# Four graph layers on one core: layer 0 without GpSimd's clearing, with signs and products a step later, and the last stores of each layer among the next layer's chunks

## The chip, the cores and the metric

The kernel runs on one core of a Trainium2 chip. A core has TensorE (matrix products; PE in the profile, PEld for its weight loads), VectorE (DVE), ScalarE (ACT), GpSimd (POOL) and SyncE (SP), each with a queue of instructions of its own that is worked through in order. Transfers are issued from the queues of SyncE and ScalarE (SPq and ACTq), a few from GpSimd. The metric is the device time of one execution in microseconds.

## The reference

x has 2708 nodes with 512 features; adj is a symmetric 2708 x 2708 matrix of int32 zeros and ones, about 2.4% ones, with ones on its diagonal. Four layers follow each other, each as x = x + layer(relu(layernorm(x)), adj):

```python
# layer 0, h = relu(layernorm(x))
out0 = relu((a.T @ h @ weight) * clip(a.sum(axis=0), 1)**-0.5)
# layer 1: each node takes its first 64 neighbors
keep = (A > 0) & (cumsum(A > 0, axis=1) <= 64)
nb_mean = keep @ h / max(keep.sum(axis=1), 1)
out1 = leaky_relu(h @ W_line.T + b_line) + leaky_relu(nb_mean @ W_nb.T + b_nb)
# layer 2: attention with 8 heads of 64 features, scores f1[n] + f2[m] where adj is set
# layer 3
out3 = relu(concat(h @ W_self + b_self, agg @ W_nb + b_nb) @ W_comb + b_comb)   # agg: mean over neighbors
```

## The kernel before, in words

Nodes are cut into 22 chunks of 126 rows (R), the last one of 62. A tile of features is a chunk by 512. Every layer begins with a dense part over the 22 chunks: load x, normalize it (VectorE's statistics, ScalarE's root), transpose it on TensorE, take relu while ScalarE copies it out of PSUM (hT), multiply by a weight. The helper `dense` gives these as stages of lags 0 to 3, and `staged` traces, for each step, every stage at its lag: load of chunk c, normalization of c-1, transposes of c-2, product of c-3. The product is kept in two parts (`halves`), so that it can be multiplied in reduced precision twice. Then comes the aggregation: columns of the adjacency matrix go in six groups of 4, 4, 4, 4, 3 and 3 chunks, and for each group all 22 row chunks are walked. A pair (g, m) of group and row chunk is a unit; a unit multiplies the halves of chunk m with the adjacency block, 2 products of 512 columns for each chunk of the group, into one PSUM tile per chunk (acc).

Layer 0 does more in its units, since it also makes what the other layers read:

- `load0` loads the block adj[m, group] as int32 into ai, four buffers deep, on SyncE's queue; for the last row chunk it first lets GpSimd clear the tile.
- `count0` (lag 3) makes ar, the block in fp32r, on VectorE (L411), for the products; ab, the block in bf16, on ScalarE (L413), two buffers deep, whose last two columns GpSimd clears (L414), since the transposing product always loads 128 columns; the running count of neighbors cum with a scan on VectorE (L418); the degree up to here, a copy of cum's last column by GpSimd (L426); and the sign of 64 neighbors less the count (L428, ScalarE), summed over the row, from which the index of the last neighbor that counts (last) is found.
- `multiply0` (lag 4) has the products with acc (L330), the transposing products of ab (L456, vT_ps), whose column of ones gives the degree by column (L459, VectorE) and whose rest ScalarE copies to vT as int8 (L468). At the middle of a group it loads the x of the group's chunks. After the last row chunk it evicts each acc: relu and scale by VectorE or ScalarE (y, L480 and L489), the sum with x by GpSimd (L492), and the store to x1 on ScalarE's queue (L99, in `move`).

During group 0 the dense part of layer 0 runs in the same steps. Between layers 0 and 1 the index last is spread over rows: 22 transposes on TensorE (L532) and copies by ScalarE to lastr (L538). Layer 1's dense part writes x1 again with its own-node term, its aggregation (`aggregate`, L330 again, with kt from lastr and vT) ends each chunk in `after1`, with a sum by GpSimd (L582) and a store to x2 on ScalarE's queue. Layer 2's dense part takes x2; there ScalarE also normalizes (hn, L199). Tiles of x come from one ring of six buffers (`load_x`); in layer 2 `count_neighbors` uses the same ring for masks, four for each of 13 row chunks. y, hn and evicted tiles share a ring of three (tag "t").

All this is traced in the order of the program, but the order within each queue is set at build time by a planner that takes ready instructions by their place in the program and the times that it expects. PSUM has eight tiles, which acc, vT_ps and the dense parts share.

Of the kernel before, what the change touches and what calls it, by code (L numbers as in the profile page):

```python
# [8 lines left out]
F32 = mybir.dt.float32  # L9
F32R = mybir.dt.float32r  # L10
BF16 = mybir.dt.bfloat16
I32 = mybir.dt.int32
# [32 lines left out]
def fast_layers(  # L45
# [43 lines left out]
    def rows(c):  # L89
        return min(R, N - c * R)  # L90
# [283 lines left out]
    with ExitStack() as ring_ctx:  # L374
# [2 lines left out]
        w0s = load_weight(weights, w0, "w0s", tag="w")  # L377
        h0 = {}
        l1_weights = []

        def product0(c, xc, hT, n):
            po = ps.tile([P, D], F32, name="h0_ps", tag="ps")
# [3 lines left out]
        with tc.tile_pool(name="l0", bufs=2) as wk:  # L386
# [3 lines left out]
            def load0(i):  # L390
                g, m = units[i]
                if i == 2 * NC:
                    l1_weights.extend(
                        load_weight(weights, w, name, tag="w")
                        for w, name in ((w_nb1T, "wn"), (w_line1T, "wl"))
                    )
                cs, n, gw = groups[g], rows(m), width(groups[g])
                ai = wk.tile([R, WG], I32, name="ai", bufs=4)
                block = adj[m * R : m * R + n, cs[0] * R : cs[0] * R + gw]
                if m == NC - 1:  # L400
                    nc.gpsimd.memset(ai[:, :gw], 0)
                    move(nc.sync, ai[TAIL : TAIL + n, :gw], block)
                move(nc.sync, ai[:n, :gw], block)
                tiles[i] = ai

            def count0(i):
                g, m = units[i]
                cs, n, gw, ai = groups[g], rows(m), width(groups[g]), tiles[i]
# [4 lines left out]
                nc.scalar.activation(ab[:n, :gw], ai[:n, :gw], AF.Square)  # L413
                nc.gpsimd.memset(ab[:n, gw : KR + P - R], 0.0)  # L414
                if gw < KR:
                    nc.vector.memset(ar[:, gw:KR].bitcast(F32), 0.0)
                cum = wk.tile([R, WG], I16, name="cum")
# [18 lines left out]
                tiles[i] = ar, ab  # L436

            def multiply0(i):
# [36 lines left out]
                for k, c in enumerate(cs):  # L475
# [14 lines left out]
                            r[:n], acc.pop(c)[:n], AF.Relu, scale=nrm[:n, k : k + 1]  # L490
                        )
                    nc.gpsimd.tensor_tensor(xc[:n], xc[:n], r[:n], ALU.add)  # L492
# [33 lines left out]
        nc.vector.tensor_scalar(last, last, float(N), 0.5, op0=ALU.add, op1=ALU.mult)  # L526

        lastr = wk.tile([R, NC * R], I16, name="lastr")
        for k in range(0, NC, KMAX):
            pt = ps.tile([P, KMAX * R], F32, name="last_ps", tag="ps")  # L530
            for c in range(k, min(NC, k + KMAX)):
                nc.tensor.transpose(  # L532
                    pt[:R, (c - k) * R : (c - k + 1) * R],
                    last[:R, c : c + 1].to_broadcast([R, R]),
                    ident[:R, :R],
                )
            w = (min(NC, k + KMAX) - k) * R
            nc.scalar.copy(lastr[:, k * R : k * R + w], pt[:R, :w])  # L538
# [34 lines left out]
        def after1(c, acc, xc):  # L573
# [229 lines left out]
    with ExitStack() as stack:  # L803
# [128 lines left out]
        def count_neighbors(i):  # L932
# [809 lines left out]
```

## Time and profile before

| | us |
|---|---|
| time, median of three runs (1892.21 to 1899.74) | 1899.61 |
| span of the profiled execution | 1891.6 |
| layer 0, group 0 with the dense part (52 to 182) | 130 |
| layer 0, groups 1 to 5 (182 to 424) | 242 |
| layer 1, dense part to 593, aggregation to 812 | 388 |
| layer 2 | 812 to about 1480 |
| layer 3 | about 1480 to 1891 |
| TensorE busy over the span | 1801.5 (95%) |

A row of the costliest groups gives the line of the kernel, engine, operation, output and inputs with their shapes, the number of executions; then the busy time and the mean of one in ns; then the time that the engine sat idle just before, and what ended most of it. A row of the timeline gives start and length in us, the engine, line, operation, output and input, the count, and in brackets the idle time before it with what released it. A transfer's row lasts as long as its issues stand on the queue, waits between them included.

### The profile page before, as it was taken

The page shows a single profiled execution, that of the slowest core. Times are in us where ns is not written, and L with a number is a line of the kernel's source. Part 1 is how long each engine was busy: PE and PEld are TensorE (multiplying, and loading weights), DVE is VectorE, ACT ScalarE, POOL GpSimd, SP SyncE. Part 2 cuts the span into 40 slices and gives each one's busy share as a digit, 9 for nine tenths or more (in the row PEclk, how much of TensorE's full clock was granted, in tenths as well). Part 3 has the DMA queues.
Part 4 walks back from the last instruction along what each step waited for, and adds up shares of the span by engine and source line. Part 5 has one row for each costly group of instructions (what it writes and reads, how often), then busy time and mean ns, then how long its engine had stood idle before and what let it go on. Part 6 is the DMA issues. An engine that isn't in the chain of part 4 may idle for free.

```text
span 1891.6 us, 30561 instructions
## 1 busy us (share of the span) xinstructions
PE 1801.5 (95%) x11670; PEld 1061.5 (56%) x11670; DVE 1289.1 (68%) x1812; ACT 903.2 (48%) x1533; POOL 280.9 (15%) x461
## 2 busy tenths in 40 slices
PE   8999899989999999989899999999999799999998
PEld 4556666664446888744344453444444355478886
DVE  4655677784444556766799979999999776524333
ACT  2445777772110000047587898767777766400000
POOL 0101232331111111237600000000000222100000
PEclk9999999999999999989999999999999899999999
DMA  6333455542223111243311212211211444302321
GB/s 221 115 87 96 140 149 154 142 117 73 75 68 97 44 44 47 76 136 107 101 46 34 57 46 57 59 39 29 59 31 41 123 137 137 97 20 81 115 65 41
DMA packets 126041, 160.92 MB, mean 85 GB/s; under 512 B 57406, under 2 KB 77994, under 8 KB 125002
## 3 DMA queue, kind: packets, MB, share of 16 engines
q1 hardware_dynamic: 106764, 123.40, 22.8%
q10 hardware_dynamic: 18544, 33.37, 5.3%
q0 software_dynamic: 576, 2.10, 0.3%
q8 instruction: 94, 1.54, 0.3%
q14 instruction: 63, 0.52, 0.1%
HBM read 111.23 MB, written 47.42 MB: 84 GB/s over the span
## 4 chain that ended last, share of the span: by engine, by line
PE 74%; DVE 7%; DMA 5%; issue 5%; ACT 5%; POOL 2%; SPq 0%; ACTq 0%; DVEq 0%; POOLq 0%
PE acc L330 27%; PE av L882 15%; PE nb_ps L182 8%; PE sums L882 5%; DVE t L858 4%; PE self_ps L182 4%; PE line_ps L182 4%; PE h_ps L182 4%; PE wh_ps L182 3%; DMA ai<-in_adj 2%; PE hT_ps L210 2%; DMA x<-x 1%; DVE cum L418 1%; POOL x L492 1%; ACT sign L428 1%
## 5 line engine op out<-in xcount | busy, mean ns | idle before, releaser
L858 DVE SCALAR_TENSOR_TENSOR t<-rb,ec,vT 126x2708 f32<-126x2708 f32 (+2 forms) x220 | 528.1, 2467 | 25.2 <-ACT b L843 11.0
L882 PE MATMUL av<-t,whs 126*32 126x451 f32 (+4 forms) x4576 | 443.1, 518 | 8.6 <-ACT whs L831 7.4
L330 PE MATMUL acc<-halves,kt 126*126 126x512 f32 x1848 | 430.5, 394 | 1.1 <-DVE kt L1096 1.1
L330 PEld LDWEIGHTS acc<-halves,kt 126*126 126x126 f32 x1848 | 344.0, 186 | 85.6 <-DVE kt L1096 1.2
L843 ACT ACTIVATE b<-t,eb 126x2708 bf16<-126x2708 f32 (+5 forms) x130 | 272.5, 2096 | 39.5 <-DVE t L858 38.4
L882 PEld LDWEIGHTS av<-t,whs 126*32 126x32 f32 (+1 forms) x4576 | 170.6, 110 | 202.0 <-issue 159.8
L330 PE MATMUL acc<-halves,ar 126*126 126x512 f32 x924 | 254.1, 415 | 8.9 <-ACT ab L413 4.3
L330 PEld LDWEIGHTS acc<-halves,ar 126*126 126x126 f32 x924 | 166.5, 189 | 52.8 <-issue 11.6
L563 DVE SCALAR_TENSOR_TENSOR kt<-lastr,index,vT 126x504 fp32r<-126x504 int16 (+1 forms) x132 | 104.3, 798 | 82.1 <-PE acc L330 81.8
L1096 DVE CAST kt<-vT 126x504 fp32r<-126x504 int8 (+1 forms) x132 | 52.7, 400 | 140.8 <-PE acc L330 140.8
L191 ACT ACTIVATE ln_rs<-ln_mv,eps 126x1 f32<-126x1 f32 x88 | 25.5, 294 | 257.6 <-DMA x<-x 202.8
L418 DVE TENSOR_TENSOR_SCAN cum<-ai,deg 126x504 int16<-126x504 int32 (+2 forms) x110 | 125.0, 1143 | 26.9 <-DMA ai<-in_adj 13.9
L784 POOL TENSOR_SCALAR z<-y 126x512 f32<-126x512 f32 x22 | 43.1, 1957 | 646.6 <-DVE y L777 578.2
L428 ACT ACTIVATE sign<-cum,limit 126x504 bf16<-126x504 int16 (+3 forms) x132 | 88.5, 671 | 59.2 <-DVE cum L418 53.9
L882 PE MATMUL sums<-t,whs 126*32 126x339 f32 (+3 forms) x1152 | 107.7, 455 | 5.7 <-ACT out L921 5.7
L831 ACT ACTIVATE whs<-wh,ef 126x64 f32<-126x64 f32 x220 | 73.7, 341 | 69.4 <-PE sums L882 35.5
L212 ACT ACTIVATE hT<-hT_ps 128x504 f32<-128x504 f32 x88 | 51.4, 587 | 103.4 <-PE hT_ps L210 99.4
L187 DVE BATCH_NORM_STATS2 ln_st<-x 126x6 f32<-126x512 f32 x88 | 60.4, 687 | 58.2 <-DMA x<-x 46.0
L468 ACT CAST vT<-vT_ps 126x504 int8<-126x504 f32 (+1 forms) x132 | 70.9, 539 | 47.4 <-DVE sums L459 24.1
L182 PE MATMUL nb_ps<-wn,hT 128*126 128x512 f32 x176 | 81.9, 609 | 2.6 <-ACT hT L212 2.6
L182 PE MATMUL wh_ps<-w2s,hT 128*126 128x512 f32 (+1 forms) x176 | 80.9, 603 | 0.0
L182 PE MATMUL nb_ps<-wfn,hT 128*126 128x512 f32 x176 | 80.4, 600 | 0.0
(172 smaller groups left out, 2054.2 us busy)
## 6 DMA issues: line engine op xcount, KB each, us to landing
x<-x SPq DMA_DIRECT2D x105, 252.0 KB
x<-x ACTq DMA_DIRECT2D x84, 252.0 KB
ai<-in_adj SPq DMA_DIRECT2D x84, 248.1 KB
x<-in_x SPq DMA_DIRECT2D x42, 252.0 KB
rb<-rT SPq DMA_DIRECT2D x7, 1332.8 KB
wh<-whd SPq DMA_DIRECT2D x70, 94.5 KB
whd<-wh SPq DMA_DIRECT2D x21, 252.0 KB
aT<-avT SPq DMA_DIRECT2D x21, 252.0 KB
```

The lines of the kernel that those rows point to most:

```text
L182: nc.tensor.matmul(po[:n], lhsT[:, f, :n], w[:, f, :], start=(f == 0), stop=(f == NF - 1))
L187: nc.vector.bn_stats(st[:n], xc[:n])
L330: nc.tensor.matmul(acc[:R], weight[:, k * R : (k + 1) * R], parts[:, i, :], start=(m == 0 and i == 0), stop=(m == NC - 1),)
L418: nc.vector.tensor_tensor_scan(cum[:n, :gw], ai[:n, :gw], ai[:n, :gw], 0.0 if g == 0 else deg[:n, m : m + 1], op0=ALU.add, op1=ALU.max,)
L428: nc.scalar.activation(sign[:n, :gw], cum[:n, :gw], AF.Sign, bias=limit[:n], scale=-1.0, accum_out=signs[:n, m, g : g + 1],)
L468: nc.scalar.copy(vT[g][:, :, m * R : (m + 1) * R], pt[:R, :K, :R])
L563: nc.vector.scalar_tensor_tensor(by_chunk(kt, cs), lastr[:, cs[0] * R : (cs[-1] + 1) * R].rearrange("p (c r) -> p c r", r=R), index[:R, m ...
L831: nc.scalar.activation(t[:q, :O], wh.pop((u, m))[:q], AF.Copy, scale=by)
L843: nc.scalar.activation(b[:q, : hi - lo], weight[s][:q, : hi - lo], AF.Sigmoid, bias=eb[:q, m, h : h + 1], scale=STEEP,)
L858: nc.vector.scalar_tensor_tensor(t[:q, : hi - lo], row[h][:q, lo:hi], ec[:q, m, h : h + 1], vT[g][:q, k, lo:hi], op0=ALU.max, op1=ALU.mult,)
L882: nc.tensor.matmul(p[j * S : j * S + lhsT.shape[1], : b - a], lhsT, rhs[:, part * size + a : part * size + b], start=(m == 0), stop=(m == ...
L1096: nc.vector.tensor_copy(by_chunk(kt, cs), pattern(m, cs))
```

## The change

In layer 0 the block is loaded two columns wider where there are any, so that ab's two extra columns are made by ScalarE with the rest and GpSimd clears them only in the last group. ai goes from four buffers to five, ab from two to three. The copy of the degree moves from GpSimd to VectorE. The sign is written over cum and goes into a stage of its own. Counts, signs and products have lags 4, 5 and 6, where counts had 3 and products 4. The sums of a group are kept (`sums1`), and their stores to x1 are traced in the steps of row chunks 1 to 4 of the next group; those of the last group among the chunks of layer 1's dense part, those of layer 1's last group among layer 2's. The spreading of last goes among layer 1's chunks too. To make room, the ring of x has five buffers, not six. The purpose is that ScalarE's queue does not hold stores that wait for GpSimd in front of work that TensorE needs, and that GpSimd's adds do not hold ab.

```diff
-    def load_x(src, c, name="x", pool=None, bufs=6, twice=False):
+    def load_x(src, c, name="x", pool=None, bufs=5, twice=False):
...
+        def save2(c):
+            move(nc.scalar, x2[c * R : c * R + rows(c), :], sums1.pop(c)[: rows(c)])
+        def save1(c):
+            move(nc.scalar, x1[c * R : c * R + rows(c), :], sums1.pop(c)[: rows(c)])
...
-                ai = wk.tile([R, WG], I32, name="ai", bufs=4)
+                wide = min(gw + P - R, N - cs[0] * R)
+                ai = wk.tile([R, WG + P - R], I32, name="ai", bufs=5)
...
-                ab = wk.tile([R, WG + P - R], BF16, name="ab")
-                nc.scalar.activation(ab[:n, :gw], ai[:n, :gw], AF.Square)
-                nc.gpsimd.memset(ab[:n, gw : KR + P - R], 0.0)
+                ab = wk.tile([R, WG + P - R], BF16, name="ab", bufs=3)
+                nc.scalar.activation(ab[:n, :wide], ai[:n, :wide], AF.Square)
+                if wide < KR + P - R:
+                    nc.gpsimd.memset(ab[:n, wide : KR + P - R], 0.0)
...
-                nc.gpsimd.tensor_copy(deg[:n, m : m + 1], cum[:n, gw - 1 : gw])
-                sign = wk.tile([R, WG], BF16, name="sign", bufs=1)
+                nc.vector.tensor_copy(deg[:n, m : m + 1], cum[:n, gw - 1 : gw])
+                tiles[i] = ar, ab, cum
+
+            def sign0(i):
...
                 nc.scalar.activation(
-                    sign[:n, :gw],
+                    cum[:n, :gw],
                     cum[:n, :gw],
                     AF.Sign,
...
-                    move(nc.scalar, x1[c * R : c * R + n, :], xc[:n])
+                    sums1[c] = xc
+
+            def save0(i):
+                g, m = units[i]
+                if g and 1 <= m <= len(groups[g - 1]):
+                    save1(groups[g - 1][m - 1])
...
-                (3, count0),
-                (4, multiply0),
+                (4, count0),
+                (5, sign0),
+                (6, save0),
+                (6, multiply0),
...
-        for k in range(0, NC, KMAX):
+        def spread_last(k):
+            if k % KMAX:
+                return
...
-        staged(NC, *dense(x1, product1))
+        def save_last(c):
+            if c < len(groups[-1]):
+                save1(groups[-1][c])
+        staged(NC, *dense(x1, product1), (3, save_last), (4, spread_last))
...
-            move(nc.scalar, x2[c * R : c * R + n, :], xc[:n])
+            sums1[c] = xc
+            if c not in groups[-1]:
+                save2(c)
...
-    staged(NC, *dense(x2, product2, False, [(4, sums2), (5, rows2)], scalar=True))
+    def save_last2(c):
+        if c < len(groups[-1]):
+            save2(groups[-1][c])
+    more = [(3, save_last2), (4, sums2), (5, rows2)]
+    staged(NC, *dense(x2, product2, False, more, scalar=True))
...
-                t = common.tile([P, D], F32, name="x", bufs=6).bitcast(BF16)
+                t = common.tile([P, D], F32, name="x", bufs=5).bitcast(BF16)
```

More of the change, by code (lines that the diff above doesn't have):

```diff
@@ L379, in fast_layers @@
         l1_weights = []
+        sums1 = {}
+        def save2(c):
+            move(nc.scalar, x2[c * R : c * R + rows(c), :], sums1.pop(c)[: rows(c)])
+        def save1(c):
+            move(nc.scalar, x1[c * R : c * R + rows(c), :], sums1.pop(c)[: rows(c)])
         def product0(c, xc, hT, n):
@@ L397, in load0 @@
                 cs, n, gw = groups[g], rows(m), width(groups[g])
-                ai = wk.tile([R, WG], I32, name="ai", bufs=4)
-                block = adj[m * R : m * R + n, cs[0] * R : cs[0] * R + gw]
+                wide = min(gw + P - R, N - cs[0] * R)
+                ai = wk.tile([R, WG + P - R], I32, name="ai", bufs=5)
+                block = adj[m * R : m * R + n, cs[0] * R : cs[0] * R + wide]
                 if m == NC - 1:
[L401 to L404, printed above, removed]
+                    nc.gpsimd.memset(ai[:, :wide], 0)
+                    move(nc.sync, ai[TAIL : TAIL + n, :wide], block)
+                move(nc.sync, ai[:n, :wide], block)
+                tiles[i] = ai, wide
             def count0(i):
                 g, m = units[i]
-                cs, n, gw, ai = groups[g], rows(m), width(groups[g]), tiles[i]
+                cs, n, gw, (ai, wide) = groups[g], rows(m), width(groups[g]), tiles[i]
                 KR = len(cs) * R
@@ L411, in count0 @@
                 nc.vector.tensor_copy(ar[:, :gw], ai[:, :gw])
-                ab = wk.tile([R, WG + P - R], BF16, name="ab")
-                nc.scalar.activation(ab[:n, :gw], ai[:n, :gw], AF.Square)
-                nc.gpsimd.memset(ab[:n, gw : KR + P - R], 0.0)
+                ab = wk.tile([R, WG + P - R], BF16, name="ab", bufs=3)
+                nc.scalar.activation(ab[:n, :wide], ai[:n, :wide], AF.Square)
+                if wide < KR + P - R:
+                    nc.gpsimd.memset(ab[:n, wide : KR + P - R], 0.0)
                 if gw < KR:
                     nc.vector.memset(ar[:, gw:KR].bitcast(F32), 0.0)
-                cum = wk.tile([R, WG], I16, name="cum")
+                cum = wk.tile([R, WG], I16, name="cum", bufs=2)
                 nc.vector.tensor_tensor_scan(
@@ L425, in count0 @@
                 )
-                nc.gpsimd.tensor_copy(deg[:n, m : m + 1], cum[:n, gw - 1 : gw])
-                sign = wk.tile([R, WG], BF16, name="sign", bufs=1)
+                nc.vector.tensor_copy(deg[:n, m : m + 1], cum[:n, gw - 1 : gw])
+                tiles[i] = ar, ab, cum
+            def sign0(i):
+                g, m = units[i]
+                n, gw = rows(m), width(groups[g])
+                ar, ab, cum = tiles[i]
                 nc.scalar.activation(
-                    sign[:n, :gw],
+                    cum[:n, :gw],
                     cum[:n, :gw],
@@ L492, in multiply0 @@
                     nc.gpsimd.tensor_tensor(xc[:n], xc[:n], r[:n], ALU.add)
-                    move(nc.scalar, x1[c * R : c * R + n, :], xc[:n])
+                    sums1[c] = xc
+            def save0(i):
+                g, m = units[i]
+                if g and 1 <= m <= len(groups[g - 1]):
+                    save1(groups[g - 1][m - 1])
             def first_dense(lag, fn):
```

## The prediction

> **What bounds the kernel now.** I read the page first: shares of busy time, the chain that ended last, the costliest groups.
>
> ```profile
> PE 1801.5 (95%) x11670; PEld 1061.5 (56%) x11670; DVE 1289.1 (68%) x1812; ACT 903.2 (48%) x1533; POOL 280.9 (15%) x461
> PE 74%; DVE 7%; DMA 5%; issue 5%; ACT 5%; POOL 2%; SPq 0%; ACTq 0%; DVEq 0%; POOLq 0%
> ```
>
> TensorE is busy for 95% of the span, so no edit here can gain more than the holes in it. The next view is the busy time by stage. Layer 0 walks six groups of columns; the five rows are its groups 1 to 5. Columns: stretch, its length, then busy time of TensorE, its weight loads, VectorE, ScalarE, GpSimd.
>
> ```profile
> 182.00:233.00 51.00, 45.61 (x247) 33.42 (x248) 35.95 (x65) 36.07 (x81) 15.00 (x43) 1.00 0.52 148
> 233.00:287.00 54.00, 49.55 (x271) 35.72 (x269) 42.04 (x74) 41.59 (x94) 16.40 (x52) 1.00 0.52 152
> 287.00:334.00 47.00, 43.67 (x239) 31.90 (x240) 36.20 (x68) 37.74 (x88) 14.12 (x49) 1.00 0.50 145
> 334.00:381.00 47.00, 42.67 (x226) 30.40 (x225) 37.13 (x79) 36.56 (x99) 15.77 (x54) 0.96 0.51 144
> 381.00:424.00 43.00, 38.74 (x219) 27.80 (x217) 34.66 (x116) 33.85 (x100) 14.37 (x50) 1.00 0.40 113
> ```
>
> TensorE stands idle for 5.4 + 4.5 + 3.3 + 4.3 + 4.3 = 21.8 us of these 242. Between the boundaries of groups it does not: the stretch 312 to 334 has 22.00 busy of 22.00. So the loss hangs on the boundaries. The timeline of the first one shows how:
>
> ```profile
> 185.08 4.87 POOL L492 TENSOR_TENSOR x<-x,y 126x512 f32<-126x512 f32 x3 [0.82 <-ACT y L489]
> 186.40 6.04 ACTq L99 DMA_DIRECT2D x<-x  x4
> 190.04 0.23 PE L456 MATMUL vT_ps<-ident,ab 126*128 126x128 bf16 x1 [0.34 <-POOL ab L414]
> 192.48 1.06 ACT L468 CAST vT<-vT_ps 126x504 int8<-126x504 f32 x2 [6.26 <-POOL ab L414]
> 194.12 0.40 PE L456 MATMUL vT_ps<-ident,ab 126*128 126x128 bf16 x4 [1.95 <-ACT ab L413]
> 203.99 0.40 PE L456 MATMUL vT_ps<-ident,ab 126*128 126x128 bf16 x4 [1.12 <-ACT ab L413]
> ```
>
> GpSimd adds the residual of four chunks (185.1 to 192.1). The four stores of x1 stand on ScalarE's queue and each waits for its add, so ScalarE does nothing from 186.2 to 192.5: the 6.26 in brackets. GpSimd's clearing of ab (L414) is merely the last semaphore that the profile names; the adds hold it too. Without ScalarE no ab is made and TensorE waits 1.95 us. The hole at 203.99 is its echo: the ai buffers were freed late and the loads of x for the next group stood ahead of ai on SyncE's queue until the stores landed (the chain there reads add, store of x 4.49 us, load of ai 5.10 us, scan, sign, ab).
>
> Holes of at least 0.15 us, summed from the same view: 9.1 us directly at the five boundaries (194.12 and its like at 245.9, 250.1, 300.8, 350.7, 389.9, with the small waits for L414) and 12.2 us of echoes, late loads and the ends of groups (204.0, 218.4, 287.9, 339.6, 354.9, 395.2 and others).
>
> At the start of layer 0:
>
> ```profile
> 49.74 3.60 PE L182 MATMUL h_ps<-w0s,hT 128*126 128x512 f32 x8
> 50.00 0.59 ACT L212 ACTIVATE hT<-hT_ps 128x504 f32<-128x504 f32 x1 [3.25 <-PE hT_ps L210]
> 57.61 3.75 PE L330 MATMUL acc<-halves,ar 126*126 126x512 f32 x8 [4.27 <-ACT ab L413]
> 62.44 4.07 PE L182 MATMUL h_ps<-w0s,hT 128*126 128x512 f32 x8
> ```
>
> hT of chunk 2 is ready at 50.6, yet TensorE waits from 53.3 to 57.6 for the first adjacency, because the product of step 4 stands ahead of chunk 2's dense product (62.44). Then the passages into layers 1 and 2:
>
> ```profile
> 427.24 2.30 ACT L538 CAST lastr<-last_ps 126x504 int16<-126x504 f32 x5 [3.78 <-POOL x L492]
> 430.08 6.34 PE L182 MATMUL nb_ps<-wn,hT 128*126 128x512 f32 x8 [2.63 <-ACT hT L212]
> 815.61 1.99 ACTq L99 DMA_DIRECT2D x<-x  x2
> 817.64 0.81 ACT L199 ACTIVATE hn<-x,ln_shift,ln_rs 126x512 f32<-126x512 f32 x1 [19.90 <-DMA x<-x]
> 821.22 5.26 PE L182 MATMUL wh_ps<-w2s,hT 128*126 128x512 f32 x8
> ```
>
> In both, ScalarE first sits behind stores (and behind five copies of lastr), then makes what TensorE waits for.
>
> **What the Trainium skill says.** "DMA: Bandwidth & Descriptors", Anatomy of one DMA: a semaphore wait of a transfer happens on the issuing sequencer, before dispatch. The trace agrees: 6.26 us of a dead ScalarE. "GPSIMD Engine Reference", Specifications: GpSimd's SBUF interfaces are shared with VectorE, with contention for two-port modes. It agrees: the cast to ar takes 0.40 us alone and 1.33 while an add runs (384.27, 387.08). "TensorE: Matmul & The Clock Gate", Part 1: after an idle window the clock is half until about 3.4 us of activity. It agrees in kind: eight products took 3.75 us after the hole of 4.27 and 1.85 later.
>
> **The change, part by part.**
>
> *Stores of layer 0's chunks at steps 1 to 4 of the next group.* Same number of stores. A store is now traced two or more units behind its add; one unit gives ScalarE three instructions, 1.68 us back to back (sign 0.70, ab 0.53, copy of vT 0.45 from start to start). First store about 2 × 1.68 = 3.4 us after the ys (185.6), so near 189.0, the others one unit (2.15 us) apart; the adds end near 186.3, 187.9, 189.9, 192.1. No store should wait. Of the 9.1 us I take 75%, 6.8.
>
> *No clearing by GpSimd, ab three deep, ai five deep, signs a step later.* 110 of 132 clearings go (the last group keeps its 22). They cost 0.10 us on an idle engine; what counts is that ab no longer stands behind adds. ai five deep and products two steps behind the counts give one more unit of lead (2.15 us, or 1.63 in groups of three chunks) against late loads. The sign waited 14.2 us for scans in this stage and blocked ab behind it; a step later the scan is done. Of the 12.2 us of echoes I take 45%, 5.5: the loads of x still go on SyncE's queue behind stores, now with one buffer fewer.
>
> *The degree's copy goes from GpSimd to VectorE.* 132 copies of one column. Bounds: 0.10 us (the shortest four-column copy, L459) to 0.25 (one dependent small step to the next, 418.47 to 418.72); I take 0.16. In 356 to 380, about 15 units, VectorE is busy 20.18 of 24.00; 15 × 0.16 = 2.4 more makes 94%. It fits, but with casts slowed by adds VectorE recovers more slowly after a boundary. Cost 0 to 5 us, taken as 1. Two more columns of ai and ab are nothing.
>
> *Products at step 6.* Chunk 2's dense product now comes ahead of the first adjacency product and fills the hole at 53.3; half clock after it (3.75 instead of 1.85) goes too. 0 to 6 us; I take 4.
>
> *lastr and the last stores among layer 1's chunks.* The first hT is ready for ScalarE at 425.98 (transposes end) instead of 429.38, so the first product could begin near 426.6, not 430.1: 3.5 us. Against it the 22 transposes of last (2.53 us), now hidden in a hole at 421.3, may fall among products that leave TensorE no gap. Between -1 and 4, taken as 2.5.
>
> *The last stores of layer 1 among layer 2's chunks.* hn(0) can start when the first add ends, 815.5, and not at 817.64. But x is five deep: three chunks wait for their store, so x of chunk 2 can only be loaded once the first is stored; today it was loaded near 788. Store near 816.4, landed 2.9 us later, load and statistics 3.7 us: 823.0, transposed by 825.5, about when TensorE asks for it (826). Between -3 and 4, taken as 1.5.
>
> *x five deep elsewhere.* In layer 2 the counting of neighbors copies four masks per step into x buffers, 13 times, while ScalarE is busy 58.8 of 60 us (1066 to 1126). One buffer less can hold a copy back: 0 to 3 us lost, taken as 1. In layers 1 and 3 a buffer is held five steps of 7.3 and 7.9 us with a load of 3.7 us; hidden behind the products.
>
> Sum: 6.8 + 5.5 + 4 + 2.5 + 1.5 - 1 - 1 = 18.3 us. 1899.6 - 18.3 = **1881 us**.
>
> **Rivals.** (a) *Only the blocked ScalarE is cured*, 1894: 6.8 us of it, while loads of ai stay behind loads of x on SyncE's queue, the start is as before, and the passages cancel: about 6 us. For it: late loads end 16.0 us of VectorE's waits for ai in the stage, and a fifth ai buffer lengthens no queue ahead. Against: those loads were late mostly because ScalarE freed ai late.
> (b) *VectorE or the shorter ring of x becomes the bound, slower*, 1908: copies at 0.25 us make a unit of three chunks 1.40 + 0.25 = 1.65 us against TensorE's 1.63, so nothing is caught up after a boundary (5 us), the passages lose 3 + 1 and the masks 3; the cured stores give back 4: net +8. For it: VectorE's 84% in that stretch. Against: four of six groups have 2.15 us per unit.
> (c) *All holes close*, 1866: 21.8 + 6 + 4 + 4, less 2, is 34 us. Against: y's and slowed casts still come at each boundary.
>
> **Numbers.** Forecast 0.63, (a) 0.20, (b) 0.10, (c) 0.07. Range 1867 to 1897: from near (c) to past (a), leaving out most of (b) and the far side of (c). Faster by over 0.5% (under 1890.1): nearly all of the forecast, (c) and a little of (a), 0.70. Within 0.5%: 0.21. Slower: 0.09.
>
> **What would show it.** Right: no ScalarE hole of over 2 us at the five boundaries, TensorE's idle time in groups 1 to 5 near 9 us, dense products back to back from 45.8, first nb_ps by 427 counted from the same end of layer 0. Wrong: VectorE over 93% busy with TensorE waiting for ar; SyncE's queue stalled on x with ai behind it; hn(2) of layer 2 late by the deferred store; masks spread out in layer 2. The order within each queue is chosen by a planner at build time, which draws ready instructions forward (reductions of layer 3, L1071, run at 421 us); its reaction to the new steps is the largest unknown.

## The result, and the profile after

The changed kernel takes 1878.38 us (median of four runs, 1876.26 to 1880.16); beside it the kernel before takes 1897.97 us (now a median of four, 1892.21 to 1899.74). The ratio is 0.9902, with a 95% interval of 0.9876 to 0.9927: 1.0% faster. The forecast was 1881 us.

The busy times of the kernel after:

```profile
PE 1803.5 (96%) x11670; PEld 1057.0 (56%) x11670; DVE 1302.2 (69%) x1944; ACT 900.5 (48%) x1533; POOL 234.5 (13%) x219
```

TensorE makes the same products in a span of 1874.1 instead of 1891.6 us: 17.5 us less. Its idle time falls from 90.1 to 70.6 us, and its busy time is 2 us longer. VectorE has 132 instructions more, the copies of the degree, of about 0.15 us each; its busy time grows by 13 us. The busy time by stage, the same five groups of layer 0, cut near the start of each group's last products (columns as before: stretch, length, TensorE, its weight loads, VectorE, ScalarE, GpSimd):

```profile
180.00:228.40 48.40, 46.74 (x261) 34.27 (x259) 40.81 (x90) 37.73 (x86) 7.19 (x6) 1.00 0.52 152
228.40:278.10 49.70, 47.80 (x263) 34.43 (x261) 42.55 (x94) 40.06 (x92) 7.19 (x6) 1.00 0.54 156
278.10:327.70 49.60, 47.66 (x263) 34.42 (x261) 41.34 (x94) 39.28 (x92) 7.18 (x6) 1.00 0.51 151
327.70:367.70 40.00, 37.88 (x198) 26.33 (x197) 35.04 (x94) 32.61 (x91) 7.01 (x8) 0.96 0.54 155
367.70:404.20 36.50, 35.81 (x196) 25.55 (x195) 32.50 (x124) 30.23 (x93) 7.94 (x26) 1.00 0.43 118
```

TensorE is idle for 1.7 + 1.9 + 1.9 + 2.1 + 0.7 = 8.3 us of them; it was 21.8, or 21.5 when the kernel before is cut at the same places. VectorE is at most 89% busy (32.50 of 36.50). The timeline of the first boundary shows what became of the blocked ScalarE:

```profile
185.35 0.38 PE L471 MATMUL vT_ps<-ident,ab 126*128 126x128 bf16 x4 [0.91 <-ACT y L504]
185.38 6.36 POOL L507 TENSOR_TENSOR x<-x,y 126x512 f32<-126x512 f32 x4 [2.05 <-ACT y L504]
187.65 1.57 ACTq L99 DMA_DIRECT2D x<-x  x2
189.26 1.06 ACT L483 CAST vT<-vT_ps 126x504 int8<-126x504 f32 x2 [2.82 <-DVE deg L436]
```

GpSimd's four adds take 6.36 us, where they took 7.0. ScalarE's hole is 2.82 us and not 6.26, but it is not cured: two of the four stores still stand in front and wait for their adds (the row at 187.65, which ends at 189.22, and ScalarE goes on at 189.26). The other two go out at 190.70 and 192.28, behind their adds and among ScalarE's other work. At the five boundaries ScalarE's longest holes were 6.26, 5.75, 5.38, 5.22 and 4.04 us; they are 2.82, 2.87, 2.87, 1.88 and 2.09. By the profile TensorE now waits here for ScalarE's copies to vT and its y's, 6.9 us of about 8; these free PSUM tiles (0.91 above). For ab it waits 0.2 us, where it waited 13.0.

TensorE's timeline at the start of layer 0:

```profile
53.48 3.60 PE L182 MATMUL h_ps<-w0s,hT 128*126 128x512 f32 x8
...
71.73 0.65 PE L210 MATMUL hT_ps<-ident,hn 126*128 126x126 f32 x4 [1.47 <-ACT vT L483]
```

The hole of 4.27 us and the half clock after it are gone, but group 0 ends only 2.4 us earlier, since a new hole comes at 71.73, where TensorE waits for a copy to vT, and smaller ones follow: between 62 and 100 TensorE is busy for 36.30 of 38 us, where it was busy throughout.

The passages into layers 1 and 2:

```profile
406.49 3.88 POOL L507 TENSOR_TENSOR x<-x,y 126x512 f32<-126x512 f32 x3 [0.85 <-ACT y L504]
409.40 1.07 PE L210 MATMUL hT_ps<-ident,hn 126*128 126x126 f32 x4 [4.20 <-DVE hn L201]
...
798.54 0.81 ACT L199 ACTIVATE hn<-x,ln_shift,ln_rs 126x512 f32<-126x512 f32 x1 [17.85 <-POOL x L612]
801.98 6.18 PE L182 MATMUL wh_ps<-w2s,hT 128*126 128x512 f32 x8
808.20 0.59 ACT L693 COPY wh<-wh_ps 126x512 f32<-126x512 f32 x1 [4.36 <-PE wh_ps L182]
809.74 0.65 PE L210 MATMUL hT_ps<-ident,hn 126*128 126x126 f32 x4 [1.57 <-ACT hn L199]
```

In both, TensorE first waits for GpSimd's adds (406.49 and, by the bracket, at 798.54); the first dense product then begins some 2 us earlier than it did, counted from the end of the layer ahead. At 809.74 TensorE waits for the third chunk's hn. Its x isn't what is late: it was loaded from 799.38 on, right behind hn(0) and before the first store went out (800.31), and its statistics are ready at 805.5. But ScalarE stands for 4.36 us in front of the copy of the first product (808.20), and makes this hn only behind it, at 808.88.

Where the 17.5 us came from, read from the starts of the first or last products of each stage, in one profile of each kernel:

| stage | before | after | gain | forecast |
|---|---|---|---|---|
| start to the end of group 0 | 182.03 | 179.67 | 2.4 | 4 |
| layer 0, groups 1 to 5 | 238.42 | 224.56 | 13.9 | 6.8 + 5.5 - 1 |
| last product of layer 0 to first product of layer 1's aggregation | 171.73 | 170.96 | 0.8 | 2.5 |
| that product to the first attention product of layer 2 | 326.9 | 326.0 | 0.9 | 1.5 |
| that product to layer 3 | 572.0 | 572.3 | -0.3 | -1 |
| layer 3, to the last store | 395.9 | 396.0 | -0.2 | 0 |

How far such a difference can be trusted shows in the kernels below, where most of these stages are alike. Groups 1 to 5 take 222.9 to 224.6 us in four kernels whose layer 0 is that of the kernel after (in one of them with other adds in the last group). The third row is 171.0 to 171.7 us in the four kernels that have this passage as before, and 169.9 to 171.9 in the seven that have it as after: its 0.8 isn't resolved. The fourth row is 326.7 to 328.1 us in four and 324.7 to 326.0 in eight: there the late stores bring 1.5 us by the means, more than this pair shows.

### The profile page after: what moved, and what is told of

Same layout as the page of the kernel before. It is cut to its first block, busy times and chain, and to the rows that moved or that the text cites. A ratio compares the mean times of both kernels' runs of the same rounds, so it can differ in the third digit from the quotient of the medians.

```text
span 1874.1 us, 30317 instructions
## 1 busy us (share of the span) xinstructions
PE 1803.5 (96%) x11670; PEld 1057.0 (56%) x11670; DVE 1302.2 (69%) x1944; ACT 900.5 (48%) x1533; POOL 234.5 (13%) x219
## 4 chain that ended last, share of the span: by engine, by line
PE 65%; DVE 12%; issue 5%; ACT 4%; DMA 3%; POOL 0%; SPq 0%; DVEq 0%; ACTq 0%; POOLq 0%
PE acc L330 25%; PE av L919 12%; PE nb_ps L182 8%; DVE t L895 7%; PE self_ps L182 4%; PE line_ps L182 4%; PE sums L919 4%; PE wh_ps L182 4%; DVE cum L428 3%; PE hT_ps L210 2%; DMA rb<-rT 1%; DMA ai<-in_adj 1%; ACT cum L443 1%; ACT b L880 1%; ACT x L978 1%
## 5 line engine op out<-in xcount | busy, mean ns | idle before, releaser
L443 ACT ACTIVATE cum<-cum,limit 126x504 int16<-126x504 int16 (+3 forms) x132 | 88.4, 670 | 65.4 <-DVE deg L436 63.4
L182 PE MATMUL h_ps<-w0s,hT 128*126 128x512 f32 x176 | 80.1, 598 | 0.9 <-ACT hT L212 0.9
```

The source lines that it names most:

```text
L182: nc.tensor.matmul(po[:n], lhsT[:, f, :n], w[:, f, :], start=(f == 0), stop=(f == NF - 1))
L443: nc.scalar.activation(cum[:n, :gw], cum[:n, :gw], AF.Sign, bias=limit[:n], scale=-1.0, accum_out=signs[:n, m, g : g + 1],)
```

## The experiments

Each was timed beside the kernel before, whose single times went from 1890.64 to 1901.92 us; ratios are to it, in brackets the 95% interval. "Groups" is the time of groups 1 to 5 of layer 0 in the profile (before 238.4 us, after 224.6), "group 0" its time from the first dense product to its last product (before 136.3, after 134.0); the first dense product itself comes between 43.8 and 47.8 us in these kernels, ahead of anything that the edits touch.

**The stores, taken back from the change, and alone.** After, with the stores of groups 0 to 4 at once behind their adds:

```diff
                     sums1[c] = xc
+                    if g < len(groups) - 1:
+                        save1(c)
...
-                (6, save0),
```

> The changed kernel, but layer 0 traces the stores of groups 0 to 4 at once behind their adds, as before; the last group's stay late. Theory (ScalarE held by waiting stores is the larger part): the five groups 1 to 5 take about 231 us, not 224.6, and the time is about 7 us over the changed kernel's, near 1885. Rival (deeper buffers and later products absorb the blocked ScalarE, so where the stores stand no longer matters): within 2 us of the changed kernel.

Measured: 1888.32 us, ratio 0.9959 (0.9948 to 0.9971); groups 235.2. The timeline of its first boundary has the blocked ScalarE back:

```profile
189.02 4.41 ACTq L99 DMA_DIRECT2D x<-x  x4
193.48 1.06 ACT L483 CAST vT<-vT_ps 126x504 int8<-126x504 f32 x2 [5.67 <-DVE sums L474]
```

Before, with nothing changed but that these stores are made at the next group's first steps:

```diff
-                    move(nc.scalar, x1[c * R : c * R + n, :], xc[:n])
+                    if g == len(groups) - 1:
+                        move(nc.scalar, x1[c * R : c * R + n, :], xc[:n])
+                    else:
+                        sums1[c] = xc
...
                 (3, count0),
+                (4, save0),
                 (4, multiply0),
```

> The kernel before, with nothing but the stores of groups 0 to 4 moved to row chunks 1 to 4 of the next group (at lag 4, with the products). Theory: groups 1 to 5 fall from 238.4 to about 231 us, the time to about 1891. Rival: under 2 us gained, since GpSimd's clearing and the short buffers still hold ab.

Measured: 1884.40 us, ratio 0.9938 (0.9916 to 0.9961); groups 227.7. Its first boundary:

```profile
191.16 0.13 DVE L460 COPY sums<-vT_ps 126x4 f32<-126x4 f32 x1
191.32 0.58 ACT L469 CAST vT<-vT_ps 126x504 int8<-126x504 f32 x1 [3.09 <-DMA x<-x]
```

ScalarE still stands for 3.09 us there, half of what it was; at the other four boundaries its longest holes are 1.3 to 2.0 us. The bracket names a store, but none stands on ScalarE's queue in this hole: the second went out at 188.06, the next at 193.06. The copy to vT begins 0.03 us after VectorE's copy of the sums ends (191.16), which stood behind two scans of 3.70 us. TensorE's waits for ab between 182 and 420 us (sum, times, longest):

```profile
PE vT_ps L457 <- POOL ab L415: 5.3, 4, 2.1
PE vT_ps L457 <- ACT ab L414: 3.0, 5, 1.0
```

The two agree: the late stores are worth 238.4 - 227.7 = 10.7 us of the groups alone and 235.2 - 224.6 = 10.6 us within the whole change, both more than the 7 us that were expected. All the rest brings some 3 us there. The waits left for ab are 5.3 us behind GpSimd's clearing, which stands behind the adds, and 3.0 behind ScalarE.

**The steps.** After, with counts, signs and products at the lags of before:

```diff
-                (4, count0),
-                (5, sign0),
-                (6, save0),
-                (6, multiply0),
+                (3, count0),
+                (3, sign0),
+                (4, save0),
+                (4, multiply0),
```

> The changed kernel with counts and signs at lag 3 and products and stores at lag 4, as before; buffers, engines and late stores stay. Theory: group 0 loses its 2.4 us at the start and the groups lose a part of their lead, 1 to 3 us: 3 to 5 us slower, near 1883. Rival (the later step is the whole gain): 10 us slower or more.

Measured: 1887.02 us, ratio 0.9955 (0.9942 to 0.9967); group 0 140.1 (6.1 us longer than after), groups 229.6 (5.1 longer): between theory and rival. TensorE's timeline:

```profile
58.90 3.75 PE L330 MATMUL acc<-halves,ar 126*126 126x512 f32 x8 [4.27 <-ACT ab L422]
187.18 1.82 PE L330 MATMUL acc<-tail,ar 126*126 126x512 f32 x4 [3.46 <-DVE tail L254]
```

The hole at the start is back, to a hundredth the one of before, with its half clock (3.75), and a second one stands at the end of group 0, where the product waits for the last chunk's tail. The later steps are what fills the first hole.

**GpSimd's two jobs.** After, with both back on GpSimd, then one at a time:

```diff
-                wide = min(gw + P - R, N - cs[0] * R)
+                wide = gw
...
-                if wide < KR + P - R:
-                    nc.gpsimd.memset(ab[:n, wide : KR + P - R], 0.0)
+                nc.gpsimd.memset(ab[:n, gw : KR + P - R], 0.0)
...
-                nc.vector.tensor_copy(deg[:n, m : m + 1], cum[:n, gw - 1 : gw])
+                nc.gpsimd.tensor_copy(deg[:n, m : m + 1], cum[:n, gw - 1 : gw])
```

Both:

> The changed kernel with both small jobs given back to GpSimd: clearing of ab's last columns (and narrow loads), and the degree's copy. Theory (with ab three deep they stand off the path except behind the adds): 1 to 4 us slower. Rival (the clearing behind the adds is what held ab, the stores only looked like it): 7 us slower or more, with ScalarE or TensorE waiting for the clearing at every boundary. A third way: faster, if the 132 copies on VectorE cost more than GpSimd's.

Measured: 1898.28 us, ratio 1.0012 (1.0003 to 1.0021). All of the gain is gone, far more than was expected; group 0 takes 146.2 and the groups 235.7. The clearing alone (the first two parts of the diff):

> After, but GpSimd clears the last columns of ab again in every unit (and the loads of ai are narrow again); the degree's copy stays on VectorE. Theory A (what the prediction said: the clearing costs 0.10 us on an idle engine and is merely named as the last semaphore; with ab three deep it is not waited for except behind the adds): within 3 us of the kernel after, 1878 to 1882; group 0 as after (end near 180), groups 1 to 5 at most 2 us longer. Theory B (GpSimd's queue, in order, behind adds and anything that waits, holds ab at each boundary and TensorE with it): 1885 to 1892, the loss at the five boundaries, group 0 unchanged.

Measured: 1879.77 us, ratio 0.9915 (0.9898 to 0.9931); group 0 134.4, groups 225.4: as after, theory A. The copy alone (the last part):

> After, but the degree's copy of one column is done by GpSimd again; no clearing. Theory A (the copy on VectorE is a cost of 132 x 0.07 to 0.16 us, partly on the path): 1877 to 1879, not slower than after. Theory B (the sign overwrites cum, so ScalarE must now wait until GpSimd has read the degree's column, and GpSimd's queue waits for the scan and stands behind the adds): about 1890, with waits of ScalarE for the degree's copy, as in the kernel that has both GpSimd jobs back, which stood at 1898. If both jobs on GpSimd are needed for that loss, neither this nor the one with the clearing alone goes past 1884.

Measured: 1898.02 us, ratio 1.0011 (1.0004 to 1.0018); group 0 145.2, groups 237.1. So one copy of one column, 0.15 us on VectorE, costs some 20 us if GpSimd makes it, 132 times. The timeline of a step of group 0 shows the loop of waits that it stands in. The copy on GpSimd:

```profile
101.87 0.32 SPq L99 DMA_DIRECT2D ai<-in_adj  x1
104.88 1.21 DVE L428 TENSOR_TENSOR_SCAN cum<-ai 126x504 int16<-126x504 int32 x1 [1.52 <-DMA ai<-in_adj]
106.15 0.18 POOL L436 CAST deg<-cum 126x1 f32<-126x1 int16 x1 [6.71 <-DVE cum L428]
106.37 0.72 ACT L443 ACTIVATE cum<-cum,limit 126x504 int16<-126x504 int16 x1 [3.20 <-POOL deg L436]
107.08 0.57 ACT L249 CAST halves<-h_ps 126x512 fp32r<-126x512 f32 x1
107.68 0.69 DVE L251 TENSOR_TENSOR halves<-h_ps,halves 126x512 fp32r<-126x512 f32 x1 [1.01 <-ACT halves L249]
108.29 0.41 DVE L420 CAST ar<-ai 126x504 fp32r<-126x504 int32 x1
108.77 0.32 SPq L99 DMA_DIRECT2D ai<-in_adj  x1
```

The kernel after, the copy on VectorE:

```profile
101.51 0.32 SPq L99 DMA_DIRECT2D ai<-in_adj  x1
102.70 0.59 ACT L249 CAST halves<-h_ps 126x512 fp32r<-126x512 f32 x1
104.70 1.21 DVE L428 TENSOR_TENSOR_SCAN cum<-ai 126x504 int16<-126x504 int32 x1 [1.70 <-DMA ai<-in_adj]
105.94 0.15 DVE L436 CAST deg<-cum 126x1 f32<-126x1 int16 x1
106.01 0.68 DVE L251 TENSOR_TENSOR halves<-h_ps,halves 126x512 fp32r<-126x512 f32 x1
106.61 0.41 DVE L420 CAST ar<-ai 126x504 fp32r<-126x504 int32 x1
107.54 0.32 SPq L99 DMA_DIRECT2D ai<-in_adj  x1
```

In both the scan is drawn forward to the newest block, as soon as its load has landed, and the next load waits for the cast of an older block. With the copy on GpSimd the dense product's eviction (halves, L249) stands behind the sign on ScalarE, the sign behind the copy, the copy behind the scan, and VectorE's second half of the eviction and the cast behind that: 6.90 us from load to load. In the kernel after the eviction comes ahead of the sign (102.70) and nothing on VectorE waits for ScalarE: 6.03 us, with TensorE near full. Both the wait of the sign and the order had changed, so two more runs take them apart.

**The sign in a tile of its own, or over cum.** After, with the copy on GpSimd, and the sign out of cum (one buffer less of a small tile makes the room):

```diff
+                sign = wk.tile([R, WG], I8, name="sign", bufs=1)
                 nc.scalar.activation(
-                    cum[:n, :gw],
+                    sign[:n, :gw],
                     cum[:n, :gw],
                     AF.Sign,
...
-                nc.vector.tensor_copy(deg[:n, m : m + 1], cum[:n, gw - 1 : gw])
+                nc.gpsimd.tensor_copy(deg[:n, m : m + 1], cum[:n, gw - 1 : gw])
...
-                    sums[g] = wk.tile([R, KMAX, NC], F32, name="sums")
+                    sums[g] = wk.tile([R, KMAX, NC], F32, name="sums", bufs=1)
```

> After with the degree's copy back on GpSimd, and the sign written to a tile of its own (one byte per element; the small tile of sums is single to make room) instead of over cum, so that ScalarE's sign no longer waits for GpSimd's copy. Theory C (the loss of the kernel with the degree back, 1898, comes from the sign that must wait for GpSimd's copy, because it overwrites what that copy reads): 1878 to 1883, group 0 ending near 180. Rival D (it comes from the order in which the queues are laid out when the copy leaves VectorE: the eviction of the dense product stands behind the sign on ScalarE, and the load of the next adjacency waits for a cast behind it, a loop of 6.9 us instead of 5.97): 1893 to 1899, group 0 ending near 192.

Measured: 1887.77 us, ratio 0.9964 (0.9945 to 0.9983), between both theories; group 0 143.1, groups 228.1. A step of its group 0:

```profile
96.99 0.32 SPq L99 DMA_DIRECT2D ai<-in_adj  x1
100.08 1.21 DVE L428 TENSOR_TENSOR_SCAN cum<-ai 126x504 int16<-126x504 int32 x1 [1.60 <-DMA ai<-in_adj]
...
101.39 0.72 ACT L444 ACTIVATE sign<-cum,limit 126x504 int8<-126x504 int16 x1 [3.10 <-DVE cum L428]
102.10 0.57 ACT L249 CAST halves<-h_ps 126x512 fp32r<-126x512 f32 x1
103.78 0.32 SPq L99 DMA_DIRECT2D ai<-in_adj  x1
```

The sign no longer waits for GpSimd (101.39, released by the scan), but the eviction still stands behind it, and from load to load it is 6.79 us. And before, with the sign over cum as its one edit:

```diff
-                sign = wk.tile([R, WG], BF16, name="sign", bufs=1)
                 nc.scalar.activation(
-                    sign[:n, :gw],
+                    cum[:n, :gw],
                     cum[:n, :gw],
```

> Before, with one edit: the sign overwrites cum. The degree's copy stays on GpSimd, all else as before. Theory C (overwriting makes ScalarE wait for GpSimd's copy, which stands behind the adds at each boundary): slower than before by 3 to 15 us. Rival D (the order of the queues matters, not this wait): within 3 us of before, 1893 to 1899.

Measured: 1910.58 us, ratio 1.0080 (1.0058 to 1.0103); group 0 141.8, groups 247.0. Theory C here. ScalarE's longest waits between 44 and 440 us, in the kernel before:

```profile
ACT sign L428 <- DVE cum L418: 53.9, 38, 2.9
```

and in this one:

```profile
ACT cum L427 <- POOL ab L414: 62.0, 28, 4.6
ACT cum L427 <- POOL deg L426: 17.1, 24, 3.3
```

The sign waits for GpSimd, 79.1 us in all, where it had waited for the scan (53.9) and but once for GpSimd (4.0). The first row names the clearing of ab, which the sign doesn't read; in group 0 the clearing stands right behind the copy on GpSimd (102.41 and 102.30), and the sign begins 0.04 us after the copy's end. Last, before with the degree's copy on VectorE as its one edit:

```diff
-                nc.gpsimd.tensor_copy(deg[:n, m : m + 1], cum[:n, gw - 1 : gw])
+                nc.vector.tensor_copy(deg[:n, m : m + 1], cum[:n, gw - 1 : gw])
```

> Before, with one edit: the degree's copy of one column on VectorE. The sign has its own tile, so nobody waits for the copy but the next group's scan. By the prediction (the copy costs 0 to 5 us, taken as 1, and brings nothing alone): 1896 to 1899. Rival (the copy on VectorE brings the changed order of the queues by itself, and the start of layer 0 with it): 1888 to 1893.

Measured: 1894.41 us, ratio 0.9998 (0.9989 to 1.0007); group 0 135.9, groups 236.3. Alone it brings and costs nothing that the time shows.

| sign | degree's copy on | rest as | ratio |
|---|---|---|---|
| own tile | VectorE | before | 0.9998 |
| over cum | GpSimd | before | 1.0080 |
| over cum | VectorE | after | 0.9902 |
| own tile | GpSimd | after | 0.9964 |
| over cum | GpSimd | after | 1.0011 |

Writing the sign over cum saves a tile, and where GpSimd makes the copy it has a price: 0.8% in the kernel before, and about 0.5% in the kernel after (the last two rows). That it is free where VectorE makes the copy isn't shown, since the kernel after was not run with a tile of its own for the sign and the copy on VectorE. In the kernel after, GpSimd's copy costs 1.1% (0.9902 to 1.0011). About 0.5% of it is the sign's wait for it: that shows in the groups, 237.1 against 228.1, where the copy stands behind the adds. (The run with the sign apart also has one buffer less of the sums; whether that costs something wasn't tested.) The other 0.6% stays when the sign is apart, and shows most in group 0, 143.1 against 134.0, where the order of the queues is the other one. The place of the eviction alone doesn't do that. A step of group 0 in the kernel before:

```profile
99.98 0.32 SPq L99 DMA_DIRECT2D ai<-in_adj  x1
104.14 0.71 ACT L428 ACTIVATE sign<-cum,limit 126x504 bf16<-126x504 int16 x1 [2.47 <-DVE cum L418]
104.85 0.56 ACT L249 CAST halves<-h_ps 126x512 fp32r<-126x512 f32 x1
105.32 0.62 ACT L413 ACTIVATE ab<-ai 126x504 bf16<-126x504 int32 x1
105.97 0.32 SPq L99 DMA_DIRECT2D ai<-in_adj  x1
```

Here too the eviction stands right behind the sign, and yet it is 5.99 us from load to load: the load waits for ab on ScalarE. In the two kernels with 6.79 and 6.90 us it waits for the cast, which stands behind VectorE's half of the eviction. So eviction and cast together make the long loop, which is read from the timelines and not shown by a run of its own. Why the planner puts the eviction behind the sign in the new steps when the copy leaves VectorE isn't settled.

**The passages.** After, with both as before (stores at once, limits spread before the dense part), and x five deep as after:

```diff
-        staged(NC, *dense(x1, product1), (3, save_last), (4, spread_last))
+        for c in groups[-1]:
+            save1(c)
+        for k in range(0, NC, KMAX):
+            spread_last(k)
+        staged(NC, *dense(x1, product1))
...
-            if c not in groups[-1]:
-                save2(c)
+            save2(c)
...
-    more = [(3, save_last2), (4, sums2), (5, rows2)]
+    more = [(4, sums2), (5, rows2)]
```

> After, but both layer passages as before: the last chunks of layers 0 and 1 are stored at once behind their adds, and the limits are spread over the 22 chunks before layer 1's dense part. From the comparison of the stages the two passages brought 0.8 us each: 1880 (theory A: shifted work, gains 2.1 us at each passage's start, given back by transposes among the products and by a late third x). By the prediction's terms (2.5 + 1.5): 1882.5. Rival: they cost more than they bring with the ring of x at five, then 1876 to 1878.

Measured: 1882.44 us, ratio 0.9927 (0.991 to 0.9943). After, with only the limits before layer 1's dense part again:

```diff
-        staged(NC, *dense(x1, product1), (3, save_last), (4, spread_last))
+        for k in range(0, NC, KMAX):
+            spread_last(k)
+        staged(NC, *dense(x1, product1), (3, save_last))
```

> After, but the 22 transposes and six copies of the limits stand before layer 1's dense part again, where TensorE has a hole, while the last stores of layers 0 and 1 stay late. Theory A (TensorE waits 4.20 us for the add behind hn there anyway, so the transposes are free there, and cost 1.4 us among the products): 1876 to 1878, dense part of layer 1 near 162.1 us and its first product at the same place. Rival (the copies of the limits on ScalarE come ahead of hT and push the first product back by 3 us, as before): 1880.

Measured: 1877.95 us, ratio 0.991 (0.9893 to 0.9926): in the range of theory A, but not to be told from the kernel after by time. And this, with the adds of the last group on VectorE, in layers 0 and 1:

```diff
-                    nc.gpsimd.tensor_tensor(xc[:n], xc[:n], r[:n], ALU.add)
+                    eng = nc.vector if g == len(groups) - 1 else nc.gpsimd
+                    eng.tensor_tensor(xc[:n], xc[:n], r[:n], ALU.add)
...
-            nc.gpsimd.tensor_tensor(xc[:n], xc[:n], y[:n], ALU.add)
+            eng = nc.vector if c in groups[-1] else nc.gpsimd
+            eng.tensor_tensor(xc[:n], xc[:n], y[:n], ALU.add)
             sums1[c] = xc
```

> A version meant to be better than after: the limits are spread before layer 1's dense part again, and the residual adds of the last group of layers 0 and 1 are done by VectorE, not GpSimd (an add of 126x512 is 1.3 to 1.6 us there, about 0.7 on VectorE). Theory A (the first chunks of layers 1 and 2 wait for these adds): first dense product 1 to 2 us earlier in each passage, 1874 to 1877. Rival (VectorE makes the normalized chunks too and is the one to wait for, so the adds only change places): 1877 to 1880.

Measured: 1872.81 us, ratio 0.9873 (0.9854 to 0.9892), a little below theory A. Its passages:

```profile
404.25 2.53 PE L559 MATMUL last_ps<-ident,last 126*126 126x126 f32 x22
405.65 1.89 DVE L508 TENSOR_TENSOR x<-x,y 126x512 f32<-126x512 f32 x3
408.05 1.17 PE L210 MATMUL hT_ps<-ident,hn 126*128 126x126 f32 x8 [1.27 <-DVE hn L201]
```

The three adds take 1.89 us together where GpSimd's took 3.88, the first dense product comes at 409.38, 5.0 us after layer 0's last product ends, and the 22 transposes lie in a wait that is there anyway. By stage, in us:

| | before | after | both as before, x five deep | limits early | limits early, adds on VectorE |
|---|---|---|---|---|---|
| last product of layer 0 to layer 1's aggregation | 171.7 | 171.0 | 171.3 | 168.7 | 167.1 |
| that to the first attention product | 326.9 | 326.0 | 329.1 | 325.4 | 323.2 |
| that to layer 3 | 572.0 | 572.3 | 576.5 | 575.2 | 577.0 |

The first passage was worth nearly nothing as the change made it (0.3 to 0.8 us, not resolved), and 3 us with the transposes in the hole. In the second the shorter ring of x alone seems to cost 1 to 2 us (329.1 in this one profile, 326.7 to 328.1 in the four kernels with six buffers), and the late stores bring 3 to 4 us against that. The third row holds back a verdict on the totals: these three kernels are 3 to 5 us longer in layer 2, which their edits don't touch; waits of VectorE for the sums near 1260 us, of up to 3.08, are a part of it. Whether the planner's order or chance brings them isn't shown. The last version is the fastest measured, and its two passages are 3.9 and 2.8 us shorter than those of the kernel after; but its interval and that of after (0.9876 to 0.9927) overlap, so by time alone it isn't shown to be better.

## Why the prediction was right, step by step

- *Stores of layer 0, 6.8 us*: the mechanism was right, the term too small. It measured 10.7 alone and 10.6 inside the change. The direct holes were 9.1; so some of the echoes, which the prediction gave to the deeper buffers, were the stores' too. The Trainium skill's statement that a transfer's wait holds the issuing sequencer ("DMA: Bandwidth & Descriptors", Anatomy of one DMA) carried this step, and the run with the stores at once agrees: 5.67 us of dead ScalarE behind four stores. "No store should wait" did not come true, and the sign "no hole of over 2 us" was missed: 1.9 to 2.9 us are left, in which two stores still stand at the first boundary. The gain came without it, since TensorE no longer waits for ab (0.2 us, where it was 13.0).
- *No clearing, deeper buffers, later steps, 5.5 less 1 for the copy*: some 3 us in the groups, where 4.5 were forecast. Within it the later steps are what counts (5.1 us when taken back; other parts must lose some of it), and the clearing is nothing that can be resolved: 225.4 against 224.6. That the clearing "is merely the last semaphore" holds for this kernel. It doesn't where the stores alone are late and ab is two deep: there TensorE waits 5.3 us for it.
- *The degree's copy on VectorE, 1 (0 to 5)*: no cost that can be seen, 0.9998 by itself. The step left out the main thing on it: with the sign written over cum, GpSimd's copy would have stood in the way of ScalarE, and the whole gain would have been lost (1.0011). The prediction costed the move as a price, and it is the condition of another edit, the sign over cum, that it had not costed at all. That the time came out right here is luck: both edits were made together.
- *Start of layer 0, 4*: 2.4 by the profile. Right in kind, as the run with the lags of before shows by getting the 4.27 us back; the gain is in part given back at 71.73 for a PSUM tile. Six kernels with the later steps take 133.7 to 135.3 us for group 0 and three with the steps of before 135.9 to 136.6, so this term is about 2 us by the means, half of what was taken. The prediction also put the half clock's part too high: eight products at full clock take 2.41 us in this stage (in the kernel before, at 65.95), and not the 1.85 that it set against 3.75.
- *Passage to layer 1, 2.5*: 0.8 in this pair, and not resolved. The first dense product comes 6.5 us after layer 0's end and not 8.7 (5.6 was predicted: it waits for the adds, through the three buffers of y); then the dense part is 1.4 us longer for the transposes among its products, the loss that the prediction named and took as smaller.
- *Passage to layer 2, 1.5*: 0.9 in this pair, 1.5 by the means over the runs. The start comes 2.1 us earlier; then hn(2) is late, as named, but not by the deferred store: ScalarE makes it behind the copy of the first product, and the first products run 6.18 us for eight where 3.60 are usual. TensorE waits 1.57 us at 809.74.
- *Masks, -1*: -0.3 by this pair, and not resolved: layer 2 took 570.4 to 572.6 us in the four kernels with six buffers of x and 571.7 to 577.0 in the ten with five; the longer ones of these lost some of their time near 1260 us, after the masks.

The sum of the gains, 17.5 where 18.3 was predicted, hides errors of +3.9 for the stores, -1.3 for the rest of the groups, -1.6 for the start and -2.3 for the passages (and +0.5 for layers 2 and 3). That they cancel to less than 1 us is luck; what the prediction had right is where the holes were and that the blocked ScalarE was the largest of them. Rival (a), only the stores work, is the nearest to the truth of the groups, but it gave them 6 us and not 10.7.

## What to carry to other kernels

A store that waits for a slow producer belongs on its queue where the producer is done, and what it costs is its direct hole and the late buffers behind it together. Before an operand is overwritten in place, ask who else reads it and on which queue that reader stands: 132 copies of about 0.2 us cost some 20 us, not quite half of it since the overwriting instruction had to wait for them, the rest with an order of the queues that changed with them. Work that is spread "among" other work must find holes there; 22 transposes were free in a wait of 4 us, and the dense part was 1.4 us longer when they stood among its products.

## What of the hardware was not expected

- A hole costs more than its length, and the price comes late. In the kernel after, TensorE stands for 4.26 us before 799.41; the four transposes there still take their usual 0.65 us, and only then does the granted clock fall. In the rows below (columns as in the table of stages) it is the third number from the end, 1.00 at full clock:

```profile
800.00:801.00 1.00, 0.06 (x1) 0.00 (x0) 0.00 (x0) 0.78 (x2) 1.00 (x2) 0.67 0.37 113
801.00:807.00 6.00, 5.91 (x10) 2.92 (x11) 2.01 (x6) 1.39 (x4) 0.41 (x1) 0.50 0.71 218
807.00:808.00 1.00, 1.00 (x3) 0.23 (x1) 0.00 (x0) 0.00 (x0) 0.00 (x0) 0.91 0.38 76
```

By these it is half from about 800.3 to 807.2, and the eight products at 801.98 take 6.18 us against 3.60 for the next eight, at 810.23. The Trainium skill, "TensorE: Matmul & The Clock Gate", Part 1, has the half clock until about 3.4 us of activity. The trace agrees in kind, not in size: TensorE works for some 6.1 us (801.09 to 807.2) before the full clock is back, and in the kernel before for some 5.8 after its hole of 4.27 (57.61 to about 63.4; granted 0.50 from 57 to 63 and 0.80 from 63 to 64).
- A VectorE cast of 126x504 takes 0.41 us alone and 1.44 during GpSimd's adds (189.14 in the kernel after); VectorE's own three adds take 1.89 us together, against 1.3 to 2.3 us for each of GpSimd's in the kernel after. So at these boundaries the slow engine also slows the fast one.
- Layer 2, which no edit of layers 0 and 1 touches, took between 570.4 and 577.0 us in the profiles of these kernels. Changes under 5 us of the whole are better read by stage.
